# All fc_w product operands made in attention, two sets of them in idle residual buffers; two stores moved behind loads of values

## The chip, the cores and the metric

One core of one Trainium2 chip runs the whole block. The metric is device time in microseconds of one execution. The time before is the median of three runs; the profile is of one further execution.

## The reference

Eight sequences of 256 tokens, D = 512, 16 heads of 32, cross-attention over 256 context tokens, then an MLP with INNER = 2048. All in float32.

```python
x = layer_norm(hidden_states, ln1_w, ln1_b)
q = (x @ q_w + q_b)...; k = (enc @ k_w + k_b)...; v = (enc @ v_w + v_b)...
attn = softmax(where(mask, q @ k.T * scale, min))
hidden = (attn @ v) @ cproj_w + cproj_b + residual
y = gelu(layer_norm(hidden, ln2_w, ln2_b) @ fc_w + fc_b)
return hidden + (y @ proj_w + proj_b)
```

## The kernel before

**Groups and units.** The eight sequences go in four groups g = 0 to 3 of two sequences (512 tokens). Attention runs over all groups first, the MLP over all groups after it. Attention of a group is eight units u = 0 to 7 (four head groups of four heads, times two sequences). A unit computes scores (line 646), softmax on VectorE and ScalarE (664, 674), the division on GpSimd (688), transposes of the probabilities (699, 704) and the product with the values (`av`, 715). Scores and softmax run two units ahead and the division one unit ahead. Between these stand the projections of the next group (`pqT`, `pkT`, `pv`) and the output projection of an earlier one (`po`), a few pieces per unit.

**Strassen.** Every large matrix product (the projections, fc_w, proj_w) uses the seven-product Strassen-Winograd form on 2 by 2 blocks. An operand is a tile of seven quarters: "11", "12", "21", "22" as loaded, and three sums. `A_SUMS` makes the sums of a left operand with four GpSimd or VectorE adds of 128x512:

```python
A_SUMS = (("s3", "11", "21", ALU.subtract), ("s2", "22", "s3", ALU.subtract),
          ("21", "s2", "11", ALU.add), ("s4", "12", "s2", ALU.subtract))
```

**Two levels for fc_w.** fc_w times the normalised tokens is Strassen twice: seven outer products k = 0 to 6, each of seven inner ones, so forty-nine. Each outer product k needs an inner operand of seven quarters (1,792 KB, `FC_ORDER` names it: 11, 12, s2, s3, 21, s4, 22). They are made once, from fc_w, in attention, and kept in `w2_dram`; the MLP reads the operand for (g, k) with `load_w2` into one of the weight tiles k, q, c, v that attention has left. Before the change 11, s3, s2, 21, s4 and 12 are made in attention (keys a, b, c, d, f, lines 914 to 941); 12 (key f) is made late, in groups 2 and 3, straight into tile k, and is used there as the operand of (0, 1). The operand 22 is made after attention: `left` (lines 1139 to 1144) loads its four blocks into the buffers of proj_w's sums t4 and t1, four GpSimd adds after product 0 make its sums, and these are stored for the later groups.

**Orders.** Nothing is scheduled by a tool: each engine executes in the order in which the program issues. `begin(g, u, i, f)` puts f into slot i (0 to 3) of unit u of group g, `spread` puts several, `between` holds the projections' pieces. All large transfers are issued by SyncE (SP in the profile), also strictly in order, and an issue that waits holds up all behind it. Slot 3 of a unit holds loads: `load_v(g, hg)` reads a head group's values back from `v_dram` (line 587) for the `av` products of two units, `load_qk` the queries and keys. In slot 2, `keep_first_s2` (line 885) stores four quarters of tile a, `keep_all` (893) a whole operand.

**Residual.** Per group, `load_res` reads x in four quarters into the tiles `res11` to `res22`, `bias_res` adds a bias to one on GpSimd, and `project_out` adds the projected attention there and stores the result to `hid_dram`. For group 0 the load stands at unit 0 of group 1 although it is needed in units 6 and 7. The tag `as` holds three quarters of sums of the attention output (two buffers); group 1 does not use it.

**MLP start.** `load_w2` puts (0, 0) into q and (0, 2) into c; each product ends with `load_w2` into its own tile. After product 0 come (0, 3) into q, then (0, 4), (0, 5), the proj_w quarters (`load_pw`, 3 and then 1 of 1 MB), and the operands for group 1. `load_next` (four `hm` loads) and `residual` (`resm`) stand after products 0 and 1. `made` puts the products' sums into h, in part on GpSimd, by way of two scratch halves `hs`.

Of the kernel before, what the change touches and what calls it, by code (L numbers as in the profile page):

```python
# [10 lines left out]
F32 = mybir.dt.float32  # L11
# [5 lines left out]
P = 128  # L17
# [5 lines left out]
def tile_xattn_block(  # L23
# [45 lines left out]
    nc = tc.nc  # L69

    B, S, D = x.shape
# [4 lines left out]
    NG = B // GB  # L76
# [9 lines left out]
    HI, HC, HF, HD2 = INNER // 2, NC // 2, NF // 2, D // 2  # L86
# [46 lines left out]
    QUARTERS = ("11", "12", "21", "22")  # L133
# [10 lines left out]
    def place(name, at):  # L144

        return Operand(wts.tile([P, 7, HC, S], F32, tag=f"w{at}", name=name))
# [23 lines left out]
    def rows_of(t):  # L170
        return t.rearrange("p i h s -> p i (h s)")

    def load_fc_quarter(to, n, blocks=(0, 1, 2, 3)):

        m, c = int(n[0]) - 1, int(n[1]) - 1
        src = fc_w.rearrange("(c p) n -> p c n", p=P)
        for i in blocks:
            at = m * HI + i // 2 * HI // 2
            nc.sync.dma_start(to(i), src[:, c * HC + i % 2, at : at + HI // 2])
# [5 lines left out]
    w2, w2_place = {}, {}  # L185
    w2_order = [(g, k) for g in range(NG) for k in range(7)]

    def load_w2(at):

        if not w2_order:  # L190
            return
        g, k = w2_order.pop(0)
        t = rows_of(place(f"w2_{g}_{k}", at).t)
        n = FC_ORDER[k][0]
        if n in OWN:
            load_fc_quarter(lambda i: t[:, i], n, (0, 1, 3))
            nc.sync.dma_start(t[:, 2], w2_dram[QI[n]][:, 2])
            nc.sync.dma_start(t[:, 4:7], w2_dram[QI[n]][:, 4:7])
        else:
            nc.sync.dma_start(t, w2_dram[QI[n]])  # L200
        w2[g, k], w2_place[g, k] = t, at
# [14 lines left out]
    def sum_up(eng, x, table, *which):  # L216
        for i in which:
            to, a, b, op = table[i]
            eng.tensor_tensor(x[to], x[a], x[b], op)
# [103 lines left out]
    with ExitStack() as att:  # L323
# [296 lines left out]
        def bias_res(g):  # L620

            r = res[g, "12"]
            nc.gpsimd.tensor_tensor(r, r, by_tiles(cbd), ALU.add)
# [122 lines left out]
        def begin(g, u, i, f, *args):  # L746
            aside[g, u, i].append(lambda: f(*args))

        def spread(g, places, pieces):

            for i, f in enumerate(pieces):
                begin(g, *places[min(i, len(places) - 1)], f)
# [38 lines left out]
        ALL = (0, 1, 2, 3)  # L791
# [58 lines left out]
            nc.sync.dma_start(ws["c"].t[:, 4:7], cw_dram[:, 1:])  # L850

        begin(1, 3, 2, load_c)
        spread(1, [(4, 1), (4, 2), (5, 1), (5, 2)], [lambda i=i: sum_up(GP, ws["c"], A_SUMS, i) for i in ALL])
        begin(1, 6, 3, keep_c)
        begin(2, 5, 0, reload_c)

# [11 lines left out]
        def flat(x):  # L871
            return x.rearrange("p h s -> p (h s)")
# [5 lines left out]

        def fc_load(key, n):
            if key not in fc:  # L880
                fc[key] = place(f"w2_{key}", {"c": "c", "d": "q", "f": "k"}[key])
            load_fc_quarter(lambda i: flat(fc[key].t[:, i]), n)

        def keep_first_s2():
# [10 lines left out]
        def keep_own(key, n):  # L895
            keep_sums(n, rows_of(fc[key].t))

        def s2_again():
            tiles = [work.tile([P, HC, S], F32, tag=f"res{n}", bufs=1, name=f"s2_{n}") for n in QUARTERS]
            for i in range(4):  # L900
                nc.sync.dma_start(flat(tiles[i]), s2_dram[:, i])
            fc["s2"] = Scratch(tiles, None)
# [6 lines left out]
        def split(key, *places):  # L909

            for i, *at in places:
                begin(*at, lambda i=i: sum_up(GP, fc[key], A_SUMS, i))
# [9 lines left out]
        sums("a", "a", "b", ALU.subtract, (0, 6, 2), (0, 6, 2), (0, 6, 1), (0, 7, 1))  # L922
        split("b", (2, 0, 6, 1))
        begin(0, 6, 2, keep_s3)
        begin(0, 7, 2, keep_first_s2)
        split("a", (0, 1, 1, 1), (1, 1, 1, 2), (2, 1, 1, 2), (3, 1, 2, 1))
        begin(1, 2, 2, keep_all, "a", "s2")

# [6 lines left out]
        begin(2, 2, 3, fc_load, "d", "12")  # L935
        sums("d", "d", "s2", ALU.subtract, (2, 4, 1), (2, 4, 1), (2, 4, 2), (2, 4, 2))
        split("d", (0, 2, 5, 1), (1, 2, 5, 2), (2, 2, 5, 2), (3, 2, 6, 1))
        begin(2, 6, 2, keep_all, "d", "s4")
        begin(2, 4, 3, fc_load, "f", "12")
        split("f", (0, 2, 7, 1), (1, 2, 7, 2), (2, 3, 2, 2), (3, 3, 4, 2))  # L940
        begin(3, 4, 3, keep_own, "f", "12")

        def first_w2():
            load_w2("q")
            w2[w2_order.pop(0)] = rows_of(fc["f"].t)
            w2_order.remove((0, 6))
            w2_place[0, 1] = "k"

        begin(NG - 1, 1, 0, first_w2)
        g = 1  # L950
        begin(g, 0, 3, load_res, 0, *QUARTERS)
        begin(g, 2, 2, bias_res, 0)
        g = 2
        begin(g, 0, 3, spill_att, 1)
        begin(g, 2, 3, reload_att, 1)
# [29 lines left out]
        def run(pieces):  # L985
            for p in pieces:
                p()
# [95 lines left out]
            split_y(0, y2, i)  # L1083
        run(o[4:])
        bias_res(3)
        run(later)
        load_w2("c")


    with ExitStack() as mlp:  # L1090
# [19 lines left out]
        def add(eng, to, a, b, op=ALU.add):  # L1110
            eng.tensor_tensor(to, a, b, op)  # L1111
# [11 lines left out]
        def sum_pw():  # L1123
# [10 lines left out]
                    yield  # L1134

        pw_sums = sum_pw()


        left = [
            pw[n].rearrange("p c n -> p (c n)")[:, ts(i, HC * S)]  # L1140
            for n, k in (("t4", 4), ("t1", 3))
            for i in range(k)
        ]
        load_fc_quarter(lambda i: left[i], "22")

        def some_pw(n):
            for f in zip(range(n), pw_sums):
# [5 lines left out]
        for g in range(NG):  # L1153
# [78 lines left out]
            def product(k, *sums):  # L1232


                wt, yn = w2_of(g, k), QI[FC_ORDER[k][1]]
                bank = {}

                def y_of(n):
                    if n in QUARTERS:
                        return ys[g].t[:, yn, int(n[0]) - 1, ts(int(n[1]) - 1, P)]  # L1240
                    return y2s[g][:, ("t1", "t2", "t4").index(n), yn, :]

                def sub(n, w, b, first, last):
                    if first:
                        bank[n] = bank_of(n, f"pf{n}_{k}").rearrange("p i (j s) -> p (i j) s", j=2)
                    for m in range(HF // 2):
                        mm(
                            bank[n][:, m, :],
                            wt(w)[:, ts(m, P)],
                            y_of(b),  # L1250
                            first and m == 0,
                            last,
                        )

                def u(n):
                    return us(n, f"u{n}_{k}").rearrange("p i (j s) -> p (i j) s", j=2)

                def made(cd, n, x):
                    some_gelus()
                    if k in (3, 4) and cd != "22":  # L1260
                        norm_piece()
                    if sums[0][1] is None:
                        add(V, block(sums[0][0], cd), bank[n], x)
                        return

                    r = h["s3"][:, parts[0] % 4 // 2, parts[0] % 2 * HF // 2 :][:, : HF // 2]
                    parts[0] += 1
                    add(V, r, bank[n], x)
                    for to, base in sums:
                        add(GP, block(to, cd), block(base, cd), r)  # L1270

                sub(1, "11", "11", True, False)
                u1 = u(1)
                nc.scalar.copy(u1, bank[1])  # L1274
                sub(6, "s2", "t2", True, True)
                u2 = u(2)
                add(V, u2, bank[6], u1)
                some_gelus()
                sub(7, "s3", "12", True, False)
                u3 = u(3)  # L1280
                add(V, u3, bank[7], u2)
                some_gelus()
                sub(5, "21", "t1", True, False)
                made("22", 5, u3)
                sub(1, "12", "21", False, True)
                some_gelus()
                for to, base in sums:
                    if base:
                        add(V, block(to, "11"), bank[1], block(base, "11"))
                    else:  # L1290
                        nc.scalar.copy(block(to, "11"), bank[1])
                sub(7, "22", "t4", False, True)
                made("21", 7, u2)
                sub(5, "s4", "22", False, True)
                made("12", 5, u2)
                if (g, k) in w2_place:
                    load_w2(w2_place[g, k])

            def w2_of(g, k):
                if (g, k) != (0, 6):  # L1300
                    return lambda w: w2[g, k][:, QI[w]]
                return lambda w: left[QI[w]]


            product(0, ("21", None))
            if g == 0:
                for to, a, b, op in A_SUMS:
                    add(GP, left[QI[to]], left[QI[a]], left[QI[b]], op)
                nc.sync.dma_start(w2_dram[QI["22"]][:, 2], left[2])
                for i in range(4, 7):  # L1310
                    nc.sync.dma_start(w2_dram[QI["22"]][:, i], left[i])
            load_next()
            product(1, ("11", "21"))
            gelu("11", 0)
# [147 lines left out]
```

## Time and profile before

| | |
|---|---|
| median of 3 runs | 744.34 us (744.27 to 744.46) |
| profiled execution | 743.3 us, span 741.1 us, granted TensorE clock 0.995 |
| TensorE (PE) busy | 723.8 us, 98% of the span |
| GpSimd (POOL) busy | 501.6 us, 68% |
| VectorE (DVE), ScalarE (ACT) busy | 417.9 us (56%), 321.8 us (43%) |
| DMA | 135.16 MB, mean 182 GB/s |
| attention, to the last `po` matmul | 354.2 us |
| MLP of groups 0 to 3, by the start of their first `pf` matmul | from 354.2, 457.8, 551.7, 645.6 us |

TensorE is busy almost throughout, so what a change can bring is found in the few places in which it is not, and in the places in which it is busy for longer than the same work takes elsewhere. Times are microseconds from the start of the span. In a timeline the brackets give an engine's idle time before the row and who ended it; `SPq` is SyncE issuing transfers; an issue's own duration is not the transfer's.

### The profile page before, as it was taken

What the parts mean: (1) busy time and instruction counts of PE and PEld (TensorE: products, weight loads), DVE (VectorE), ACT (ScalarE), POOL (GpSimd) and SP (SyncE); (2) the same over time, 40 slices, a digit from 0 to 9 for tenths busy, and PEclk for the clock granted to TensorE, in tenths of its full rate; (3) what the DMA queues carried; (4) which work ended last, traced back from release to release, by engine and by line L of the source; (5) the groups of instructions that cost most, each with busy time, mean ns of one, the idle gap of its engine ahead of it and who ended that gap; (6) DMA issues with size and microseconds to landing.
All of it is one profiled execution on the core that took longest, in us unless ns stands there. A gap on an engine that the chain in (4) does not pass through costs nothing.

```text
span 741.1 us, 14045 instructions
## 1 busy us (share of the span) xinstructions
PE 723.8 (98%) x5109; PEld 630.4 (85%) x5109; DVE 417.9 (56%) x1056; ACT 321.8 (43%) x904; POOL 501.6 (68%) x451
## 2 busy tenths in 40 slices
PE   9999999799999999999979999999999999999998
PEld 8888778677888777777969889998899988899986
DVE  4676756475557556879547775681166821566211
ACT  2276798566777777871122500216003170030500
POOL 3856889774686999996377980489604896047870
PEclk9999999999999999999999999999999999999999
DMA  9517564765347888543799801993018940163001
GB/s 303 184 58 236 181 201 170 245 229 160 96 156 271 274 291 284 194 158 93 257 348 367 327 0 57 343 338 130 0 57 313 341 157 0 54 253 107 1 0 58
DMA packets 74228, 135.16 MB, mean 182 GB/s; under 512 B 6788, under 2 KB 44976, under 8 KB 71472
## 3 DMA queue, kind: packets, MB, share of 16 engines
q1 hardware_dynamic: 73904, 134.24, 52.1%
q8 instruction: 41, 0.67, 0.4%
q14 instruction: 27, 0.22, 0.1%
q0 software_dynamic: 256, 0.02, 0.0%
HBM read 100.69 MB, written 33.55 MB: 181 GB/s over the span
## 4 chain that ended last, share of the span: by engine, by line
PE 90%; POOL 4%; DMA 3%; issue 2%; DVE 1%; ACT 0%; SPq 0%; POOLq 0%; DVEq 0%
PE py L1108 25%; PE pf L1108 22%; PE ppt L699 7%; PE pqT L441 6%; PE po L441 6%; PE pv L441 6%; PE pkT L441 5%; PE s L646 5%; PE av L715 4%; DMA w<-w_dram 2%; PE pkT L538 2%; DMA v<-v_dram 1%; POOL pr L688 1%; PE pxt L274 1%; PE pyt L274 1%
## 5 line engine op out<-in xcount | busy, mean ns | idle before, releaser
L1111 POOL TENSOR_TENSOR h<-h,hs 128x512 f32<-128x512 f32 x100 | 126.5, 1291 | 113.1 <-DVE hs L1111 112.8
L1108 PE MATMUL pf<-y,w 128*128 128x128 f32 x1456 | 166.3, 277 | 6.1 <-ACT u L1274 3.5
L1108 PEld LDWEIGHTS pf<-y,w 128*128 128x128 f32 x1456 | 165.2, 193 | 7.3 <-ACT u L1274 3.7
L688 POOL TENSOR_TENSOR pr<-pr,rsum 128x512 f32<-128x512 f32 x128 | 129.6, 1044 | 48.2 <-DVE rsum L686 29.5
L674 ACT ACTIVATE pr<-pr,nmax 128x256 f32<-128x256 f32 x256 | 127.7, 502 | 36.3 <-DVE nmax L664 36.2
L664 DVE CUSTOM_DVE_ANT_0 pr<-s,mb 128x256 f32<-128x256 f32 x256 | 93.5, 413 | 46.5 <-PE s L646 35.8
L1274 ACT COPY u<-pf 128x512 f32<-128x512 f32 x28 | 16.4, 584 | 200.3 <-PE pf L1108 200.3
L1108 PE MATMUL py<-pw,h 128*128 128x256 f32 x384 | 84.9, 379 | 0.0
L1108 PE MATMUL py<-pw_t,h 128*128 128x256 f32 x384 | 84.2, 379 | 0.0
L1108 PEld LDWEIGHTS py<-pw_t,h 128*128 128x128 f32 x384 | 72.7, 190 | 9.8
L1108 PEld LDWEIGHTS py<-pw,h 128*128 128x128 f32 x384 | 72.4, 190 | 9.6
L699 PEld LDWEIGHTS ppt<-ident,pr 128*128 128x128 f32 x512 | 57.4, 141 | 15.2 <-issue 7.9
L699 PE MATMUL ppt<-ident,pr 128*128 128x128 f32 x512 | 68.9, 277 | 0.3
L1111 DVE TENSOR_TENSOR resm<-py,resm 128x512 f32<-128x512 f32 (+1 forms) x21 | 13.6, 664 | 93.6 <-PE py L1108 93.6
L1218 ACT ACTIVATE h<-h,cols 128x256 f32<-128x256 f32 x128 | 52.1, 494 | 18.9 <-POOL h L1111 18.9
L1111 DVE TENSOR_TENSOR hs<-pf,u 128x512 f32<-128x512 f32 x72 | 49.5, 689 | 17.4 <-PE pf L1108 11.9
L1111 DVE TENSOR_TENSOR u<-pf,u 128x512 f32<-128x512 f32 x56 | 38.7, 691 | 33.3 <-PE pf L1108 25.1
L704 ACT COPY pt<-ppt 128x512 f32<-128x512 f32 x96 | 51.8, 573 | 7.1 <-PE ppt L699 7.1
L441 PE MATMUL pv<-vw,ctxT 128*128 128x256 f32 x224 | 52.4, 380 | 0.0
L441 PE MATMUL pqT<-xnT,qw 128*128 128x256 f32 x224 | 51.0, 379 | 0.0
L674 ACT ACTIVATION_READ_ACCUMULATOR pr<-pr,nmax 128x1 f32 x256 | 48.8, 191 | 0.0
L441 PEld LDWEIGHTS pqT<-xnT,qw 128*128 128x128 f32 x224 | 41.4, 190 | 5.0
(149 smaller groups left out, 1069.0 us busy)
## 6 DMA issues: line engine op xcount, KB each, us to landing
w<-w_dram SPq DMA_DIRECT2D x16, 1792.0 KB, 8.7
w<-in_L_xattn_fc_w_dram SPq DMA_DIRECT2D x30, 256.0 KB, 5.8
w<-w_dram SPq DMA_DIRECT2D x10, 768.0 KB, 7.2
ctx<-in_ctx_dram SPq DMA_DIRECT2D x16, 256.0 KB, 4.8
x<-in_x_dram SPq DMA_DIRECT2D x16, 256.0 KB, 4.7
v_dram<-st_v SPq DMA_DIRECT2D x16, 256.0 KB, 2.3
v<-v_dram SPq DMA_DIRECT2D x16, 256.0 KB, 4.2
resx<-in_x_dram SPq DMA_DIRECT2D x16, 256.0 KB, 5.5
```

The lines of the kernel that those rows point to most:

```text
L441: nc.tensor.matmul(bank[n][:, i, :], l[:, c, ts(i, P)], r[:, c, :], start=first and i == 0 and c == 0, stop=last and c == HC - 1, skip_gro ...
L646: nc.tensor.matmul(banks[j][:, i, :], qT[j * HD : (j + 1) * HD, b * S + i * P : b * S + (i + 1) * P], kT[j * HD : (j + 1) * HD, b * SK : ( ...
L664: nc.vector.tensor_tensor_reduce(pr[:, j, i, :], banks[j][:, i, :], mbias[g][1][:, b, :], scale=-SCALE, scalar=FLT_MAX, op0=ALU.add, op1=A ...
L674: nc.scalar.activation(pr[:, j, i, :], pr[:, j, i, :], AF.Exp, bias=nmax[:, j, i : i + 1], scale=-1.0, accum_out=sums[:, j, i : i + 1],)
L688: nc.gpsimd.tensor_tensor(pr[:, j], pr[:, j], rsum[:, j, :, None].to_broadcast([P, NQ, SK]), ALU.mult,)
L699: nc.tensor.transpose(ps[:, kc, ts(i, P)], probs[n][:, j, i, ts(kc, P)], ident)
L704: nc.scalar.copy(pt, ps)
L715: nc.tensor.matmul(av[j * HD : (j + 1) * HD, :], vs[g, hg][:, b * NK + kc, ts(j, HD)], pts[n, j][:, kc, :], start=(kc == 0), stop=(kc == N ...
L1108: nc.tensor.matmul(ps, lhsT, rhs, start=first, stop=last, skip_group_check=True)
L1111: eng.tensor_tensor(to, a, b, op)
L1218: nc.scalar.activation(h[n][:, :, p, :], h[n][:, :, p, :], AF.Gelu_apprx_tanh, bias=col(c_fcb, half * HF + p), scale=1.0,)
L1274: nc.scalar.copy(u1, bank[1])
```

## The change

1. Keys e and f: the operands 12 and 22 are both made in group 1, in the four residual tiles `res11` to `res22` and one buffer of the tag `as` (functions `lent` and `keep_lent`). Loads of 12 stand at (1, 1, 3), its sums in units 2 and 3, its stores at (1, 3, 3); 22 follows at (1, 4, 1), (1, 5, 1 and 2) and (1, 5, 3).
2. `load_res` for group 0 moves from (1, 0, 3) to (1, 6, 1), its `bias_res` from (1, 2, 2) to (1, 7, 1). The sums of cproj_w move from units 4 and 5 of group 1 to unit 4 alone.
3. `keep_first_s2` moves from (0, 7, 2) to (1, 0, 3), which is behind the loads of the first values of group 1, and `keep_all` of s4 from (2, 6, 2) to (3, 0, 0), behind those of group 3.
4. `left` is gone with its four loads, four adds and four stores in the MLP. The operand (0, 6) is loaded as all others are.
5. (0, 0) is loaded into k at (3, 0, 3) and (0, 1) into q at (3, 2, 0); (0, 2) into c is issued before the last four stores to `hid_dram` instead of after them. Each MLP product of group 0 loads into its tile: (0, 3) into k, (0, 4) into q, (0, 5) into c, (0, 6) into k.

SyncE issues eight transfers more than before: five each for (0, 1) and (0, 6), which are 1,792 KB each, less two because the sums of 22 are stored in two transfers instead of four. The other loads and stores are as many and as large as before, at other places.

```diff
-        spread(1, [(4, 1), (4, 2), (5, 1), (5, 2)], [lambda i=i: sum_up(GP, ws["c"], A_SUMS, i) for i in ALL])
+        spread(1, [(4, 1), (4, 1), (4, 2), (4, 2)], [lambda i=i: sum_up(GP, ws["c"], A_SUMS, i) for i in ALL])
...
+        def in_residual(name):
+            return [work.tile([P, HC, S], F32, tag=f"res{n}", bufs=1, name=f"{name}_{n}") for n in QUARTERS]
+
+        def lent(key, n):
+            if "e" not in fc:
+                fc["sums"] = work.tile([P, 3, HC, S], F32, tag="as", name="w2_e_sums")
+                fc["e"] = fc["f"] = Scratch(in_residual("w2_e"), fc["sums"])
+            load_fc_quarter(lambda i: flat(fc[key].first[i]), n)
+
+        def keep_lent(key, n):
+            nc.sync.dma_start(w2_dram[QI[n]][:, 2], flat(fc[key].first[2]))
+            nc.sync.dma_start(w2_dram[QI[n]][:, 4:7], rows_of(fc["sums"]))
...
-        begin(0, 7, 2, keep_first_s2)
+        begin(1, 0, 3, keep_first_s2)
...
-        begin(2, 6, 2, keep_all, "d", "s4")
-        begin(2, 4, 3, fc_load, "f", "12")
-        split("f", (0, 2, 7, 1), (1, 2, 7, 2), (2, 3, 2, 2), (3, 3, 4, 2))
-        begin(3, 4, 3, keep_own, "f", "12")
-
-        def first_w2():
-            load_w2("q")
-            w2[w2_order.pop(0)] = rows_of(fc["f"].t)
-            w2_order.remove((0, 6))
-            w2_place[0, 1] = "k"
-
-        begin(NG - 1, 1, 0, first_w2)
+        begin(3, 0, 0, keep_all, "d", "s4")
+
+        begin(1, 1, 3, lent, "e", "12")
+        split("e", (0, 1, 2, 2), (1, 1, 2, 2), (2, 1, 3, 1), (3, 1, 3, 1))
+        begin(1, 3, 3, keep_lent, "e", "12")
+        begin(1, 4, 1, lent, "f", "22")
+        split("f", (0, 1, 5, 1), (1, 1, 5, 1), (2, 1, 5, 2), (3, 1, 5, 2))
+        begin(1, 5, 3, keep_lent, "f", "22")
+        begin(3, 0, 3, load_w2, "k")
+        begin(3, 2, 0, load_w2, "q")
         g = 1
-        begin(g, 0, 3, load_res, 0, *QUARTERS)
-        begin(g, 2, 2, bias_res, 0)
+        begin(g, 6, 1, load_res, 0, *QUARTERS)
+        begin(g, 7, 1, bias_res, 0)
...
         bias_res(3)
+        load_w2("c")
         run(later)
-        load_w2("c")
...
-        left = [
-            pw[n].rearrange("p c n -> p (c n)")[:, ts(i, HC * S)]
-            for n, k in (("t4", 4), ("t1", 3))
-            for i in range(k)
-        ]
-        load_fc_quarter(lambda i: left[i], "22")
...
-                wt, yn = w2_of(g, k), QI[FC_ORDER[k][1]]
+                wt, yn = w2[g, k], QI[FC_ORDER[k][1]]
...
-                            wt(w)[:, ts(m, P)],
+                            wt[:, QI[w], ts(m, P)],
...
-                if (g, k) in w2_place:
-                    load_w2(w2_place[g, k])
-
-            def w2_of(g, k):
-                if (g, k) != (0, 6):
-                    return lambda w: w2[g, k][:, QI[w]]
-                return lambda w: left[QI[w]]
+                load_w2(w2_place[g, k])
...
-            if g == 0:
-                for to, a, b, op in A_SUMS:
-                    add(GP, left[QI[to]], left[QI[a]], left[QI[b]], op)
-                nc.sync.dma_start(w2_dram[QI["22"]][:, 2], left[2])
-                for i in range(4, 7):
-                    nc.sync.dma_start(w2_dram[QI["22"]][:, i], left[i])
```

More of the change, by code (lines that the diff above doesn't have):

```diff
@@ L880, in fc_load @@
             if key not in fc:
-                fc[key] = place(f"w2_{key}", {"c": "c", "d": "q", "f": "k"}[key])
+                fc[key] = place(f"w2_{key}", {"c": "c", "d": "q"}[key])
             load_fc_quarter(lambda i: flat(fc[key].t[:, i]), n)
@@ L896, in keep_own @@
             keep_sums(n, rows_of(fc[key].t))
+        def in_residual(name):
[8 more added lines that the diff above has]
+            nc.sync.dma_start(w2_dram[QI[n]][:, 4:7], rows_of(fc["sums"]))
         def s2_again():
-            tiles = [work.tile([P, HC, S], F32, tag=f"res{n}", bufs=1, name=f"s2_{n}") for n in QUARTERS]
+            tiles = in_residual("s2")
             for i in range(4):
```

## The prediction

> **What bounds the kernel now.** I read the busy line first: PE has 723.8 of 741.1 us, so a gain must come out of the 17.3 us in which it idles and out of places in which the same work takes it longer. Then who PE waited for, longest in total first (us, times, longest):
>
> ```profile
> PE av L715 <- DMA v<-v_dram: 5.2, 2, 4.2
> PE pf L1108 <- ACT u L1274: 3.5, 1, 3.5
> PE pf L1108 <- DMA w<-w_dram: 1.9, 2, 1.3
> ```
>
> The first waits for values, the others lie in the MLP. Why the values come late is in the waits of SyncE's queue:
>
> ```profile
> SPq L885 <- POOL w_a L907: 6.8, 1, 6.8
> ...
> SPq L587 <- DMA v_dram<-st_v: 6.1, 2, 4.3
> ```
>
> L885 is `keep_first_s2`: its store waits 6.8 us for GpSimd's last difference and holds up the value load behind it. The timeline of SP has the store at 131.39 and the load at 131.83; that of PE shows what it costs:
>
> ```profile
> 129.79 3.62 PE L441 MATMUL pqT<-xnT,qw 128*128 128x256 f32 x16
> 137.58 1.60 PE L715 MATMUL av<-pt,v 128*32 128x256 f32 x16 [4.17 <-DMA v<-v_dram]
> ```
>
> PE is done at 133.41 and idles 4.17 us. For the MLP I read the chain of waits in order of time (start, us, what):
>
> ```profile
> 354.36 15.20 PE pf L1108 x136
> 369.62 1.28 POOL pw_t L1111
> 370.96 1.27 POOL pw_t L1111
> 372.31 2.48 POOL pw_t L1111 x2
> 374.79 1.24 POOL h L1111
> ...
> 378.75 15.60 DMA w<-w_dram
> 394.39 11.89 PE pf L1108 x104
> ...
> 457.84 43.77 PE pf L1108 x392
> ```
>
> In group 0 the products run into GpSimd's four sums of `left` (`pw_t`) and a transfer of 15.6 us; in group 1 (457.84) the same 392 matmuls run through in 43.77 us. Last, the stages in windows (PE, PEld, DVE, ACT, POOL busy, clock, DMA share, GB/s):
>
> ```profile
> 137.60:149.20 11.60, 11.60 (x82) 8.90 (x82) 6.01 (x24) 6.69 (x22) 7.18 (x8) 0.85 0.74 247
> 160.10:171.00 10.90, 10.90 (x85) 8.81 (x86) 6.56 (x25) 6.91 (x22) 6.55 (x7) 1.00 0.68 241
> 354.20:407.00 52.80, 46.66 (x394) 45.71 (x393) 31.72 (x50) 12.65 (x26) 33.69 (x29) 0.97 0.93 334
> 457.80:501.60 43.80, 43.80 (x394) 43.80 (x393) 31.52 (x50) 10.34 (x22) 24.82 (x21) 1.00 0.85 311
> 466.00:482.00 16.00, 16.00 (x145) 16.00 (x145) 11.26 (x17) 4.47 (x10) 8.44 (x7) 1.00 0.99 391
> ```
>
> See the clock of 0.85 behind the wait for values, the 9.0 us between groups 0 and 1 of the MLP, GpSimd's free time in a unit of group 1, and the 391 GB/s that DMA reaches.
>
> **The change part by part.**
>
> *First values of group 1.* With `keep_first_s2` behind them, the load waits only for the last `v_dram` store, issued at about 124.2; 2.3 us to land (its row in the DMA issues) is 126.5, the load's median 3.9 us makes 130.4, wanted at 133.41. 3.0 us to spare; were the landing as slow as the slowest of these twelve loads (7.0), 0.1 late. Gain: unit 0 runs from 123.31 to 137.58, 14.27 us, against 10.10 of work; unit 1, with the same mix, takes 11.61, so 1.51 more. Sum 5.7. The 1.51 is clock: windows of 2 us show 0.50 at 138 and 0.65 at 140. The Trainium skill ("TensorE: Matmul & The Clock Gate", "Part 1: The HAM clock gate") says that an idle window of about 3.4 us halves the clock for about as long again, 1.7 us of loss; by it the gain is 5.9, by the trace 5.7. I take the trace. The moved store (1 MB) must land before GpSimd overwrites quarter "21" of tile a: issued at about 139.5 behind the x loads, landed by 146, GpSimd there at 143. Up to 3 us of wait on GpSimd, whose next division is wanted by PE over 5 us later: nothing.
>
> *First values of group 3.* The 1,792 KB store of s4 is issued at 278.41, and the last two `v_dram` stores, behind it, take 5.2 us to land. Without it 2.3: the load at 286.1 instead of 288.20, landed 2.9 later at 289.0, wanted at 290.15. Gain 8.55 - 7.43 (the unit before and after) = 1.1; clock 1.00 here, so no more. The store now stands ahead of the four `hm` loads, which VectorE wants from 295.8: value, key and query loads and the store are 2.6 MB, at 360 GB/s 7.3 us, so the first `hm` at 296 to 297. VectorE waits 0 to 1 us and has idle pieces of 0.4 and 0.7 right after; I take 0.2.
>
> *GpSimd in group 1.* Eight adds of 1.27 us (L219 rows), 10.2 us, come into units 2, 3 and 5; `bias_res`, 1.27, moves from unit 2 to 7. Busy per unit now 5.4 to 7.2 of 9.2 to 11.8 us, so unit 5, the fullest, comes to 6.0 - 2.5 (cproj_w sums moved to 4) + 5.1 = 8.6 of 10.0. Operand 12 is loaded behind ctx, keys and queries: 2.6 MB from 151.4, landed at 160 to 162, and GpSimd is free for it at 162.2 after `rstd`. New waits on SP: the load of 22 into `res21` waits for the store of 12 from it to land (2.3 us), and the store of 22 for GpSimd until 195; queued behind are a `v_dram` store that ScalarE has ready at 182 only, and `load_res`; no value load of group 1. Operand 22 lands at 183, wanted at 190. `load_res`, behind the stores, lands at 201 to 203; the add wants it at 202.8 and has 2.3 us idle behind. Nothing on the path, unless the cover fails: a division ends its first quarter 8 us ahead of its transposes, that much lateness is free.
> In unit 7 GpSimd is continuous from 207.5 to 223, so `bias_res` puts the last `hid_dram` store 1.27 later and with it, behind it on SP, the first values of group 2: issued 218.22, landed 221.5 to 221.9, wanted 222.84. New: 222.8 to 223.2. Cost 0 to 0.4, taken 0.2.
>
> *Groups 2 and 3.* Four adds (5.1 us) and `keep_own` leave a GpSimd that is full from 240 to 320, but PE is not waiting for it: 0. The five transfers of (0, 1) come at about 303, with DMA share 0.4 in that stretch, 50 us ahead of use: 0.
>
> *MLP group 0.* Gone: 52.8 - 43.8 = 9.0 us, of which 6.1 are PE's waits (1.28, 0.35, 3.48, 0.36, 0.67) and the rest the clock behind them (0.50 at 384). The four `left` adds, 1 MB of loads and 1 MB of stores leave; what is late next is a `load_w2`: three tiles rotate, so each operand is requested when a product ends and wanted 12.5 us later (6.25 us each). (0, 2) now waits on SP for the last `po` matmul, 354.2, with the four `hid_dram` stores behind it, the first 3.6 us later than before; only the last group's MLP reads them. Requests from 354.4 until product 5 starts at 385.45, in order: (0, 2), four `hid_dram` stores, (0, 3), `hm`, (0, 4), `resm`, (0, 5), which is 4 x 1.84 + 3 x 1.05 = 10.5 MB. At 391 GB/s that is 26.9 us, plus 2.2 fixed (shortest value load 2.9, less 0.7 for its bytes): landed at 383.5, 2.0 early. Then (0, 6) by 391.7: 388.2, and the first three proj_w quarters, 3.15 MB, by 396.3, VectorE wanting them at 399. Against this stands the skill's "DMA: Bandwidth & Descriptors" ("Measured"): a 1 MB transfer gets 341 GB/s. By it (0, 5) lands at 387.4, 1.9 late, and proj_w at about 402, 2.5 late, partly the same time: gain 6.5 instead of 9.0. This stretch itself averaged 334 before, but with idle DMA at 372 and 1 MB of `left` stores; the 391 stretch has the same kind of requests, so I lean to it and take 8.7. The stage from 407.0 to 457.8 is 0.7 longer than group 1's because of the proj_w sums, which stay: 0.
>
> Sum: 5.7 + 1.1 - 0.2 - 0.2 + 8.7 = 15.1. Against the profiled execution (743.3, its span and 2.2 around it) 728.2; the median of the runs is 1.04 above that one: 744.34 - 15.1 = 729.2.
>
> **The rivals.**
> - *Operands late in the MLP.* DMA at 341: 2.2 less than my 8.7, and with a wait over 3.4 us also the clock: 731 to 733. For it the 334 average, against it 391 in group 1. Chance 0.13.
> - *The value wait comes back in group 2.* If `load_res` is late as well, GpSimd's lateness grows in unit 7: 2 us of wait and 1.5 of clock: 732.7. For it the spare of only 1.3 us; chance 0.09.
> - *It does not do what it says:* the load still waits, for the landing of `v_dram` behind tile b's 1.8 MB of stores. Then 5.7 is not gained: 734.9. Against it: DMA moves 7 GB/s from 126 to 128. Chance 0.04.
> - *Slower: GpSimd held by the lent operands.* The adds stand in its order ahead of the divisions; if a load of 12 or 22 is late by more than the free 8 us, PE idles in every unit after it. It decides the sign at 8 + 15.1 = 23 us of lateness; with 30 us, 7 us slower, 751. DMA is at 0.3 to 0.7 there: chance 0.03, and 0.01 that losses just cancel.
>
> **How the numbers follow.** My forecast has 0.70, with the rivals above 1.0. The low end adds full covers (5.9 + 1.2 + 9.8): 727.4; the high end takes 4.2, 1.0 and 6.5 less 0.6 of new waits, or the late-operand and group 2 rivals: 733.2. About 0.2% (1.5 us) is what a measurement here can tell from no change; all cases but the last are beyond it: faster 0.96, same 0.01, slower 0.03.
>
> **What would show it.** Right: no PE wait for `v_dram` above 0.5 us, clock 1.00 from 130 to 145, the first `pf` of group 1 about 93.9 to 94.9 us after that of group 0 (103.6 before). Wrong: a PE wait for `w` before product 5 or 6, VectorE waiting for `pw` at the first `py`, PE waiting for GpSimd's `pr` or `v` around the start of group 2, VectorE waiting for `hm`.

## The result and the profile after

The changed kernel takes 735.57 us (median of 4 runs, 735.22 to 736.03) against 744.39 us of the kernel before on the same chip: ratio 0.9882, 95% interval 0.9865 to 0.9899. That is 8.8 us faster where 15.1 were forecast, and above the upper end of the forecast range, 733.2. The profiled execution takes 735.38 us, its span is 733.5.

First who TensorE waited for, in the kernel after:

```profile
PE pf L1118 <- DVE u L1121: 5.3, 1, 5.3
PE warm L1002 <- POOL ident masks.py:199: 1.4, 1, 1.4
```

The waits for values (5.2 us before) and for `w` are gone. In their place stands one wait of 5.3 us that the prediction does not have. The first value load of group 1 in the timeline of SyncE and the product that wants it, in the timeline of PE:

```profile
122.50 2.90 SPq L494 DMA_DIRECT2D v_dram<-st_v  x2
127.66 0.36 SPq L587 DMA_DIRECT2D v<-v_dram  x1
```

```profile
130.70 3.62 PE L441 MATMUL pqT<-xnT,qw 128*128 128x256 f32 x16
134.25 1.07 PE L715 MATMUL av<-pt,v 128*32 128x256 f32 x16
```

The load no longer stands behind a store that waits for GpSimd, and `av` follows without a gap. From the first `av` of group 0 to the last of group 3 attention takes 334.58 - 61.67 = 272.91 us, before 340.61 - 60.80 = 279.81: 6.9 us gained.

The new wait lies in product 0 of the MLP. The chain of waits in order of time (start, us, what) leads straight to it:

```profile
348.82 8.41 DMA hid_dram<-resx
358.16 35.22 PE pf L1118 x296
...
450.28 43.77 PE pf L1118 x392
```

What SyncE waited for ahead of the load of (0, 2), the issues of the load and of the stores, the end of the wait on VectorE, and its cost on TensorE:

```profile
SPq L200 <- PE po L441: 8.2, 1, 8.2
```

```profile
348.39 0.34 SPq L200 DMA_DIRECT2D w<-w_dram  x1
348.82 3.42 SPq L631 DMA_DIRECT2D hid_dram<-resx  x4
```

```profile
350.25 0.69 DVE L1121 TENSOR_TENSOR u<-pf,u 128x512 f32<-128x512 f32 x1 [1.09 <-PE pf L1118]
357.41 0.69 DVE L1121 TENSOR_TENSOR u<-pf,u 128x512 f32<-128x512 f32 x1 [6.47 <-DMA hid_dram<-resx]
```

```profile
348.19 4.63 PE L1118 MATMUL pf<-y,w 128*128 128x128 f32 x40
358.16 41.46 PE L1118 MATMUL pf<-y,w 128*128 128x128 f32 x352 [5.33 <-DVE u L1121]
```

VectorE writes the scratch tile `u3` only when a store to `hid_dram` has landed. The reason is in the memory map of the built program, which says where each tile lies: the MLP's pool takes over attention's memory, and `u3` (bytes 216960 to 219008 of a partition) lies in part on the residual tile `res11` (217472 to 219520), which the first of the four stores reads. The addresses were the same before the change, but the store was issued 3.5 us before the MLP began at 354.19:

```profile
350.73 7.50 SPq L631 DMA_DIRECT2D hid_dram<-resx  x4
```

It landed in 2.2 us, and the overlap cost nothing. Now the 1,792 KB load of (0, 2) stands ahead of it, and the load waits 8.2 us on SyncE for the last `po` matmul. The store is thus issued late, at 348.82, and then takes 8.4 us to land. From its issue to the instruction that waited for it are 8.6 us.

The 352 matmuls after the wait take 41.46 us. The 392 of group 1 take 43.77, so 352 of them 39.3: 2.1 us more go to a lower clock. In windows of the kernel after (the clock is the third column from the right):

```profile
357.00:359.00 2.00, 0.84 (x4) 0.85 (x5) 1.38 (x2) 0.00 (x0) 0.00 (x0) 0.50 0.59 206
359.00:361.00 2.00, 2.00 (x11) 2.00 (x11) 0.69 (x1) 0.00 (x0) 0.00 (x0) 0.50 0.00 0
361.00:363.00 2.00, 2.00 (x15) 2.00 (x15) 0.69 (x1) 0.00 (x0) 0.00 (x0) 0.71 0.25 43
```

The MLP of group 0, from its first `pf` matmul to the end of its last `py`, thus takes 450.28 - 348.19 = 102.1 us, against 103.6 before and 94.9 forecast. The other groups are as before: groups 1 and 2 take 93.87 us each in both kernels.

### The profile page after: what moved, and what is told of

It is laid out like the page before. It is cut to its first block, busy times and chain, and to the rows that moved or that the text cites. A ratio compares the mean times of both kernels' runs of the same rounds, so it can differ in the third digit from the quotient of the medians.

```text
span 733.5 us, 14067 instructions
## 1 busy us (share of the span) xinstructions
PE 722.2 (98%) x5109; PEld 630.2 (86%) x5109; DVE 415.4 (57%) x1056; ACT 322.3 (44%) x904; POOL 502.4 (68%) x451
## 4 chain that ended last, share of the span: by engine, by line
PE 91%; POOL 3%; issue 2%; DMA 2%; ACT 2%; DVE 0%; SPq 0%; POOLq 0%; DVEq 0%
PE py L1118 25%; PE pf L1118 23%; PE ppt L699 8%; PE pv L441 7%; PE pqT L441 7%; PE pkT L441 5%; PE s L646 5%; PE av L715 4%; PE po L441 4%; PE pkT L538 2%; POOL resx L630 1%; ACT h L1220 1%; DMA hid_dram<-resx 1%; PE pxt L274 1%; PE pyt L274 1%
## 5 line engine op out<-in xcount | busy, mean ns | idle before, releaser
L1118 PE MATMUL pf<-y,w 128*128 128x128 f32 x1568 | 177.9, 277 | 5.3 <-DVE u L1121 5.3
L1118 PEld LDWEIGHTS pf<-y,w 128*128 128x128 f32 x1568 | 177.7, 194 | 5.7 <-DVE u L1121 5.5
L441 PE MATMUL pv<-vw,ctxT 128*128 128x256 f32 x224 | 52.4, 380 | 0.0
```

Of the source, the lines that this page charges most:

```text
L441: nc.tensor.matmul(bank[n][:, i, :], l[:, c, ts(i, P)], r[:, c, :], start=first and i == 0 and c == 0, stop=last and c == HC - 1, skip_gro ...
L1118: nc.tensor.matmul(ps, lhsT, rhs, start=first, stop=last, skip_group_check=True)
```

## The experiments

Theory A: the missing part is the store of residual quarter 11, late behind the load and still reading memory that `u3` wants. Theory B: the MLP's start is short of transfer rate whatever the order. Times are medians; each ratio is to the kernel before on the same chip.

| | us | before | ratio (95% interval) |
|---|---|---|---|
| e1 load of (0, 2) last | 727.76 | 742.95 | 0.9789 (0.9769 to 0.9810) |
| e2 one store first | 727.59 | 742.95 | 0.9787 (0.9766 to 0.9807) |
| e3 `u3` elsewhere | 728.42 | 742.95 | 0.9794 (0.9770 to 0.9819) |
| e4 moved stores alone | 736.73 | 742.95 | 0.9908 (0.9887 to 0.9929) |
| e5 before, load first | 743.74 | 743.04 | 1.0011 (0.9996 to 1.0027) |
| e6 store on GpSimd's queue, late | 737.17 | 743.04 | 0.9928 (0.9911 to 0.9946) |
| e7 lent operands alone | 734.23 | 743.04 | 0.9887 (0.9870 to 0.9903) |
| e8 store on GpSimd's queue, early | 735.60 | 741.98 | 0.9910 (0.9881 to 0.9939) |

### e1: the load of (0, 2) behind the stores again

```diff
         bias_res(3)
-        load_w2("c")
         run(later)
+        load_w2("c")
```

> The changed kernel with one line moved back: the load of operand (0, 2) is issued behind the four hid_dram stores, as before the change. Theory A (the store of residual quarter 11 is queued behind the 1,792 KB load, so its landing takes 8.6 us, and the scratch tile u3 of the MLP, which lies on that quarter's memory, can be written only then): the wait of 5.3 us on u3 and the 2.1 us of lower clock behind it go, 735.6 - 7.4 = 728.2; but (0, 2) is now issued at about 352.3 and lands 7.6 to 8.2 later, at 360 to 360.5, wanted at 360.7, so up to 1 us may come back: 728 to 729. Theory B (the start of the MLP is short of transfer rate, whatever the order): the same bytes move, so 734 to 736, with the wait at another operand.

727.76 us. In the timeline of PE the 392 matmuls of group 0 run through:

```profile
348.13 44.19 PE L1118 MATMUL pf<-y,w 128*128 128x128 f32 x392
```

One line moved back gives what the changed kernel lacks. (0, 2), now issued at 352.22, takes 7.4 us to land and is not late. Theory B has no place for this: the same bytes move.

### e2: only the store of quarter 11 ahead of the load

```diff
         bias_res(3)
+        run(later[:1])
         load_w2("c")
-        run(later)
+        run(later[1:])
```

> The changed kernel, with only the store of residual quarter 11 ahead of the load of (0, 2), the other three stores behind it. Theory A: that store is ready about 3.5 us before the load can be issued and lands in about 2.3 us, so u3 is free, and (0, 2) is not later than now: 728.2, no wait on a transfer in the MLP. Theory B: 734 to 736.

727.59 us, with no wait on a transfer in the MLP. The timeline of SyncE, and how long the four stores and the loads of `hid_dram` took to land there:

```profile
344.73 0.37 SPq L631 DMA_DIRECT2D hid_dram<-resx  x1
348.38 0.34 SPq L200 DMA_DIRECT2D w<-w_dram  x1
348.77 3.46 SPq L631 DMA_DIRECT2D hid_dram<-resx  x3
```

```profile
DMA to landing us min/median/max: 2.1/9.7/12.7
```

The one store that matters is ready 3.6 us before the load can be issued; ahead of it, it lands in 2.1 us, the least of the row above. The other three remain late, and nobody waits for them. This version and e1 cannot be told apart in time; both beat the kernel before and the changed one.

### e3: the same order of transfers, u3 on other memory

```diff
+            if g == 0:
+                work.tile([P, 2, S], F32, tag="u3", bufs=1, name="u3_place")
             h = {
```

> The changed kernel with the order of all transfers as it is, but the scratch tile u3 allocated first in the MLP's pool, so that it lies on other memory; the second buffer of u2 then lies on residual quarter 11, and is first written in product 1, at about 356.5. Theory A: the stores land as late as now (8 to 9 us), u3 does not wait, u2 waits about 1 us: 728.2 to 729.5. Theory B, and a theory C (VectorE is slowed or held by the transfers themselves): no change, 734 to 736.

728.42 us. The stores are as late as in the changed kernel (8.1 us at the least), yet `u3` does not wait. The store of quarter 11, issued at 348.59, takes 9.2 us and lands at about 357.8. The second buffer of `u2`, which now lies on `res11`, is written just after that, at 358.00. In e2 it was written at 356.50, in an MLP that began 0.2 us later, so the delay is 1.7 us, and PE's wait on it is small:

```profile
PE pf L1118 <- DVE u L1121: 0.7, 1, 0.7
```

So it is the address, not the transfers as such: theory B and a VectorE that is slowed by them both fall.

### e4: the two moved stores alone

```diff
-        begin(0, 7, 2, keep_first_s2)
+        begin(1, 0, 3, keep_first_s2)
...
-        begin(2, 6, 2, keep_all, "d", "s4")
+        begin(3, 0, 0, keep_all, "d", "s4")
```

> The kernel before with only its two stores moved (four quarters of tile a, and operand s4) behind the loads of values. If the two value waits are worth what attention gained in the changed kernel (4.2 + 1.6 in group 1, 1.1 at the start of group 3): 744.4 - 6.9 = 737.5, and the MLP of group 0 stays at 103.6 us. If the gain in attention came from the operands made in group 1 or from what was taken off GpSimd: less, 740 to 744.

736.73 us, a ratio that is 6.8 us of 743. From the first to the last `av` it takes 273.31 us, 6.5 less than before. The MLP of group 0 takes 103.2 us, and its waits are much as before (3.5 on `u` by way of ScalarE, 1.5 on `w`, where it was 1.9). The two moves alone give 6.5 of the 6.9 us that attention gained in the changed kernel.

### e5: the kernel before with the load first

```diff
         bias_res(3)
-        run(later)
         load_w2("c")
+        run(later)
```

> The kernel before with only the load of (0, 2) issued ahead of the four hid_dram stores. Theory A: the store of residual quarter 11 lands about 8.6 us after 354.4 instead of at about 353, u3 waits until 363 and product 0 ends about 5.3 us later, with 2 us of clock behind it; the late operand (0, 3) and the sums of left come later too, but left's loads are not later than now, so some of the 9 us lost there overlaps: slower than before by 2 to 7, 745 to 750. Without theory A (only the changed kernel's other transfers make the stall): 743 to 744, as before or up to 1 us faster, since (0, 2) comes earlier.

743.74 us, no difference that shows. By time alone theory A would have failed here. The timeline of PE says otherwise:

```profile
355.31 4.63 PE L1108 MATMUL pf<-y,w 128*128 128x128 f32 x40
365.44 3.79 PE L1108 MATMUL pf<-y,w 128*128 128x128 f32 x16 [5.51 <-DVE u L1111]
369.02 6.49 PE L1108 MATMUL pf<-y,w_f 128*128 128x128 f32 x56
375.35 18.92 PE L1108 MATMUL pf<-y,w 128*128 128x128 f32 x168
395.08 6.52 PE L1108 MATMUL pf<-y,w 128*128 128x128 f32 x56 [0.80 <-DMA w<-w_dram]
```

The wait of theory A is there with 5.51 us, and the later ones have shrunk from 6.1 us to 0.8: the sums of `left` run from 368.73, at the end of product 0, where before they ran from 369.62, in product 2. The products take 407.69 - 355.31 = 52.4 us, before 52.8. One wait has taken the place of others. My expectation counted only part of that overlap.

### e6 and e8: the store on another queue

```diff
+                queue = nc.gpsimd if (g, n) == (3, "11") else nc.sync
-                later.append(lambda: nc.sync.dma_start(quarter_of(hid_dram[g], n), r))
+                later.append(lambda: queue.dma_start(quarter_of(hid_dram[g], n), r))
```

> The changed kernel, in which the store of residual quarter 11 of the last group is issued by GpSimd, on its own queue, behind its last bias add at about 352, while the 1,792 KB load runs (348.4 to 356.6). If the small store was late because it was behind the large load in the same queue: it lands 2 to 4 us after its issue, at 354 to 356, u3 waits 1.5 to 3.5 us less and the time is 732 to 734.5. If the transfer engines are simply full, whatever the queue: it lands about 8 us after 352, at 360, u3 waits longer, 738 to 740.

737.17 us, and `u3` written at 358.51, 6.8 us after the issue at 351.70: between the two expectations. The store lands 2.2 us after the load, which had been issued 3.4 us before it; PE waits longer than in the changed kernel, 6.5 us. In e8 the same store is issued by GpSimd just behind the load.

```diff
-                later.append(lambda: nc.sync.dma_start(quarter_of(hid_dram[g], n), r))
+                if (g, n) != (3, "11"):
+                    later.append(lambda: nc.sync.dma_start(quarter_of(hid_dram[g], n), r))
+                if (g, n) == (3, "21"):
+                    nc.gpsimd.dma_start(quarter_of(hid_dram[3], "11"), res[3, "11"])
```

> As e6, but GpSimd issues the store of residual quarter 11 behind its third residual add, at about 348.8, just after the 1,792 KB load (348.4). If queues share the transfer engines piece by piece, the store, one seventh of the load's size, lands 2 to 4 us after its issue, at 351 to 353, u3 waits under 2 us: 728 to 731. If a store that is issued after the load comes out after it on any queue: it lands with the load, at 356.5 to 358, u3 waits as in the changed kernel: 735 to 737.

The timelines of GpSimd and VectorE in e8 (the load was issued at 349.40):

```profile
349.78 0.83 POOL L634 DMA_DIRECT2D hid_dram<-resx  x1
```

```profile
358.13 0.69 DVE L1124 TENSOR_TENSOR u<-pf,u 128x512 f32<-128x512 f32 x1 [6.18 <-DMA hid_dram<-resx]
```

735.60 us with a wait of 5.0 us on TensorE: as in the changed kernel. The load took 8.4 us to land, until 357.8, and the store 8.2 us, until 358.0. A store that is issued 0.4 us after the load came out with it on either queue, so "behind it in the same queue" was too narrow. What holds it, the transfer engines or the issue by way of GpSimd, these runs do not tell.

### e7: the lent operands alone

The changed kernel with e1's edit and the two stores back at their old places:

```diff
-        begin(1, 0, 3, keep_first_s2)
+        begin(0, 7, 2, keep_first_s2)
...
-        begin(3, 0, 0, keep_all, "d", "s4")
+        begin(2, 6, 2, keep_all, "d", "s4")
```

> The changed kernel with (0, 2) issued behind the stores (as in e1) and with the two stores of tile a and operand s4 back ahead of the loads of values: what is left is the operands made in group 1 and the MLP without left. If the parts simply add: 743.0 - (743.0 - 727.8) + 6.9 = 734.7, with the wait for values of 4.2 us back and the MLP of group 0 at 94.6 us. If moving the stores was needed to make room for the lent operands (GpSimd or the queue): slower than that, 737 to 742, with waits of PE on GpSimd's divisions or on values in group 1.

734.23 us. In who PE waited for, the values are back, and of GpSimd there is only what the kernel before has too (1.4 us at the very start, 0.3 at `py`):

```profile
PE av L715 <- DMA v<-v_dram: 5.8, 2, 4.2
```

The MLP of group 0 takes 449.46 - 354.85 = 94.6 us. So the parts add: 1 - 0.9908 and 1 - 0.9887 are 0.0092 and 0.0113, together 0.0205, and e1, which has both, gained 0.0211.

## Why the prediction was wrong

- **Where it failed.** The step is the one on the order of (0, 2) and the stores: "(0, 2) now waits on SP for the last `po` matmul, 354.2, with the four `hid_dram` stores behind it, the first 3.6 us later than before; only the last group's MLP reads them." It was costed at nothing because I asked who reads what the stores write, and not who next writes what the stores read. The store's delay was mis-sized too: the 3.6 us are its issue alone; from an issue at the MLP's start it takes 8.4 us to land, in place of 2.2 from one 3.5 us before it. The price in the trace is 5.3 us of wait and 2.1 of clock, 7.4; between the ratios of the changed kernel and of e1, 0.0093, it is 6.9 us, with some 2 us of noise on it. That covers the whole shortfall of 6.3: with this one line back e1 has a ratio of 0.9789, which is 728.7 us for a kernel before of 744.4, where 729.2 was forecast.
- **First values of group 1.** 5.7 forecast; unit 0 now takes 10.04 instead of 14.27, unit 1 10.03 instead of 11.61: 5.8. The extra 1.6 was clock, between the 1.5 read from the trace and the 1.7 of the other estimate: from 130 to 145 the granted clock is now 1.00. Shown by e4 and, the other way, by e7.
- **First values of group 3.** 1.1 forecast; the unit takes 7.43 instead of 8.55. Right. VectorE waited 0.8 us for the first `hm`, inside the 0 to 1 allowed, and PE did not notice in the kernel after (in e2 the next unit, the one with the `hm` work, took 0.4 longer).
- **GpSimd in group 1.** The cover held: no unit of group 1 is longer than in the kernel before. The spare in group 2 held too, but barely: the value load was issued at 214.55, 3.4 us ahead of `av` at 217.93; before it was 4.6, so it came 1.2 later, as forecast. It landed in 3.1 us, a little faster than assumed, so 0.3 us were left and the 0.2 taken for it was not needed.
- **MLP group 0.** Gain 8.7 forecast, 1.5 measured; without the new wait 103.6 - 94.6 = 9.0 (e2 and e7). One reading of it was too large: of the 2.9 us put down to the clock, the granted clock before (0.94, 0.50 and 0.71 in the windows of 2 us from 382 on) gives about 1.7, an estimate; what the rest is, is not shown. Operands were not late anywhere. In e2 DMA moved 372 GB/s from 348.4 to 379.5, and (0, 5) landed at 378.4, 1.0 us before product 5 began. So the rate read from group 1's stretch, 391 GB/s, which had it 2.0 early, was the better guide here than the 341 of the Trainium skill ("DMA: Bandwidth & Descriptors", "Measured"), a figure for one transfer of 1 MB issued by GpSimd: by it (0, 5) would have been 1.9 us late.
- **The rivals.** "Operands late in the MLP" gave 731 to 733, nearer to the measured time than the forecast, for a reason that did not occur. Its working also has a slip: by its own numbers proj_w is 3.0 us late (402 against 399), not 2.5. None of the four was the cause.

In the profile the first `av` comes 0.9 us later than before; among the experiments it lies anywhere from 60.81 to 61.78, the changed kernel's own order at the start being that of before, so I count it as variation between executions. With it the traces close: 6.9 us gained in attention and 1.5 in the MLP of group 0, less 0.9, are 7.5 of the 7.6 us by which the span is shorter.

## What to carry to other kernels

When a transfer is moved ahead of stores, look up what the stores read and who writes that memory next; where pools succeed each other, this can be a tile of quite another stage, and the memory map tells it beforehand. A wait read off a trace is worth what the same work takes elsewhere without it, clock included: those terms held within 0.3 us (5.8 for 5.7, 1.1 for 1.1, 9.0 for 8.7). Equal times do not mean that nothing happened: in e5 a new wait of 5.5 us hid in the same total, while the old ones shrank by 5.3.

## What the hardware showed that was not expected

A 256 KB store took 2.1 us to land when it was issued 3.6 us ahead of a 1,792 KB load (e2), and 8.4 us when issued 0.4 us behind it (the changed kernel), about as long as the load itself, 8.2. Issued 0.4 us behind it on GpSimd's queue instead of SyncE's it was hardly faster: 8.2 us, with 8.4 for the load (e8).
